# State-space layers on one core: the products h*C of three channel tiles as one GpSimd instruction, and their sum two slots later

## The chip, the cores and the metric

The kernel runs on one core of one Trainium2 chip, everything in float32. The metric is the device time of one launch in microseconds (us). Before the change it is 25216.62 us, the median of three runs (25214.65 to 25219.68).

Names in the profile: PE is TensorE (PEld is its loading of weights, which overlaps with it), DVE is VectorE, ACT is ScalarE, POOL is GpSimd, SP is SyncE, whose queue issues nearly all DMAs.

## What is computed

Two layers of a visual state-space model, one after the other, on x of 8 images of 64x64 pixels with 192 channels. Each layer normalizes, projects to 384 channels, applies a 3x3 depthwise convolution, and then scans the 4096 pixels of an image in K directions (K = 2 in layer 0, K = 4 in layer 1). The core of it, for each direction:

```python
def step(h, inp):
    u_t, dl_t, B_t, C_t = inp
    dA = jnp.exp(dl_t[..., None] * As[None])
    h = dA * h + (dl_t * u_t)[..., None] * B_t[:, :, None, :]
    y = jnp.einsum('bkdn,bkn->bkd', h, C_t)
    return (h, y)
```

h has 384 channels times 16 states. The y of the directions are summed, layer-normalized, multiplied by a gate and projected back to 192 channels.

## The kernel before, in words

Each layer has a front (normalization, projection, convolution, copies to DRAM) and a scan part. The change is in the scan part only, the function `scans`.

**Steps.** A step is 512 pixels of one direction of one image, all 384 channels (three channel tiles of 128 partitions, `dt` = 0, 1, 2) and all 16 states (eight pairs, `m` = 0 to 7). Layer 0 has 8 x 2 x 8 = 128 steps, layer 1 has 8 x 4 x 8 = 256.

**Slots.** A step has 24 slots, one for each pair of a state pair and a channel tile: slot s is m = s // 3, dt = s % 3. Slots are numbered on through the steps; slot 31 of a step is slot 7 of the next one. The loop at the end of `scans` goes through all slots g and issues, in this order and into the in-order queue of each engine:

- `scan(g)`: two recurrences of 128x512 on DVE (L772), one for each state of the pair, reading the decays `da` from SBUF and the inputs `hb` from PSUM and writing the states `h`; behind them, on GpSimd, the product of these two states with C, `hc[:, dt]` from `h[:, dt]` and `cr` (L773);
- the work that two tables, L0_SLOTS and L1_SLOTS, put into this slot (below);
- `inject(g + 2)`: 16 PE instructions (L728) that make the inputs `hb` of the slot two ahead in one of two PSUM buffers, so that they can't start before the scans of slot g are done;
- `decay(g + 4)`: two exponentials on ACT (L745) into one of five buffers `da`, and in all but the first step of a direction a copy (L753) of the entry state, which GpSimd scales in `enter` (L665).

**The sum over states.** `reduce(i, m, n)` adds the products of state n of pair m into the PSUM tile `py` (three channel tiles) with 32x32 matmuls by a mask (L151, a helper). It is put at slot 3m + `slots["reduce"][n]` of its step: 3m + 5 for both n in layer 0, 3m + 5 and 3m + 6 in layer 1. `keep_y` copies `py` to SBUF on ACT (L821) and stores it, at slot 29, that is slot 5 of the next step; there is one `py`, so the next step's first sum waits for that copy. `carry` (L778, ACT, slot 3m + 3) keeps the last state of a chunk for the next one.

**What else has a place in the tables.** All other small PE products of the scan part share a single PSUM bank (tag "m"): each waits until ACT or DVE has read the one before. These are, with their slots in layer 0 / layer 1, counted from the step before the one that they serve: `x_proj` (L568) - / 1, 1, 3; `turn_b` (L594) 3 / 6 with the ACT copy `keep_b` (L605) at 4 / 8; `dt_proj` (L616) for dt = 0, 1, 2 at 7, 0, 4 / 5, 8, 10 with the ACT pass `dt_bias` (L630) at 8, 2, 5 / 6, 10, 11; `turn_delta` (L683) at 12, 15, 14 / 14, 15, 13 with the DVE product `make_dut` (L691) at 13, 17, 15 / 15, 16, 14. `add_y` (L151, not in the bank) adds the earlier directions to `py` at 12 / 13 (in one of the four directions of layer 1 at 24).

A finished image is closed in chunks, the operations `f_...`: once in two steps in layer 0, once in four in layer 1. Their PE parts (L871 gate, L896 and L911 sums, L950 output) lie in layer 0 at slots 9, 10, 18 twice, 22 twice (gate), 20 and 30 (sums), 23 and 32 (totals), 42 three times, 44, 46 twice (output); in layer 1 at 11, 12, 17, 18, 20, 22 (gate), 41 and 67, 45 and 70, 83, 84 twice, 89, 91, 94. Their DVE parts are two passes of 128x1536 (L914, L925; slots 24 and 33 / 48 and 72) and two additions (L959). On GpSimd they have three products of 128x512 (L944, `f_times`), at 38, 39, 36 / 76, 79, 72.

**Buffers.** `h` of one state pair (all three channel tiles, 128x3072) has two buffers, `hc` of the same size three, `cr` three. `load_c` (L714) loads `cr` of pair m at slot 3m - 6 and waits on the SP queue until GpSimd has read the buffer's last user, pair m - 3.

Of the kernel before, what the change touches and what calls it, by code (L numbers as in the profile page):

```python
# [8 lines left out]
F32 = mybir.dt.float32  # L9
# [6 lines left out]
P = 128  # L16
# [8 lines left out]
DT = 3  # L25
NS = 16
T = 512
# [27 lines left out]
    "turn_delta": (12, 15, 14),  # L55
    "make_dut": (13, 17, 15),
    "softplus": 10,
    "reduce": (5, 5),
    "add_y": 12,
    "add_turned": 26,  # L60
    "keep_y": 29,
    "f_norm": 8,
    "f_gate": ((9, 10), (18, 18), (22, 22)),
    "f_keep": (11, 20, 23),
# [37 lines left out]
    "turn_delta": (14, 15, 13),  # L102
    "make_dut": (15, 16, 14),
    "softplus": 11,
    "reduce": (5, 6),
    "add_y": 13,
    "add_turned": 24,
    "keep_y": 29,
    "f_norm": 6,
    "f_gate": ((11, 12), (17, 18), (20, 22)),  # L110
    "f_keep": (13, 19, 24),
# [399 lines left out]
def scans(tc, name, x_src, x_dst, xcd, xcd_col, xtd, xdd, t, dirs, rank, row_b, gate, slots, last, consts, dram):  # L511
# [5 lines left out]
    nc = tc.nc  # L517
# [27 lines left out]
    with tc.tile_pool(name=f"{name}_s1", bufs=1) as s1, tc.tile_pool(  # L545
        name=f"{name}_s2", bufs=2
    ) as s2, tc.tile_pool(name=f"{name}_psy", bufs=1, space=PSUM) as psy, tc.tile_pool(
        name=f"{name}_psh", bufs=2, space=PSUM
# [7 lines left out]
        live = {}  # L556
# [199 lines left out]
        def scan(i, s):  # L756
            m, dt = divmod(s, DT)
            b, k, cols, rev, ci, c = steps[i]
            hb, da = live[i].pop(("hb", s)), live[i].pop(("da", s))
            if dt == 0:  # L760
                live[i]["h", m] = (
                    s2.tile([P, DT, 2, T], F32, name="h"),
                    s2.tile([P, DT, 2, T], F32, name="hc", bufs=3),
                )
            h, hc = live[i]["h", m]
            for n in range(2):
                o, a = h[:, dt, n], da[:, n]
                v = hb.rearrange("p r (j n) -> p n (r j)", n=2)[:, n]
                if rev:
                    o, a, v = o[:, ::-1], a[:, ::-1], v[:, ::-1]  # L770
                init = 0.0 if ci == 0 else 1.0
                nc.vector.tensor_tensor_scan(o, a, v, init, ALU.mult, ALU.add)  # L772
            nc.gpsimd.tensor_mul(hc[:, dt], h[:, dt], live[i]["cr", m])  # L773

        def carry(i, m):
            b, k, cols, rev, ci, c = steps[i]
# [301 lines left out]
        with tc.manual_schedule(engines=ENGINES):  # L1078
            g = min(todo)
            while todo:  # L1080
                i, s = divmod(g, NSL)
                if 0 <= g < N * NSL:
                    scan(i, s)
                for f, a in sorted(todo.pop(g, []), key=lambda fa: rank_of.get(fa[0], 1.5)):
                    f(*a)
                if 0 <= g + 2 < N * NSL:
                    inject(g + 2)
                if 0 <= g + 4 < N * NSL:
                    decay(g + 4)
                g += 1  # L1090
# [113 lines left out]
```

## Time and profile before

| | |
|---|---|
| median of three runs | 25216.62 us |
| the profiled execution: its span | 25231.1 us |
| its scans, layer 0 (128 steps) | from 961.3 us to 8928 us, 62.2 us for a step |
| its scans, layer 1 (256 steps) | from 9864.6 us to 25183 us, 59.8 us for a step |
| busy, PE / DVE / ACT / POOL, 12000 to 24000 us | 11572.89 / 11429.45 / 9435.76 / 11526.37 us of 12000 |
| busy, the same, 3000 to 6000 us | 2855.39 / 2832.74 / 2388.18 / 2833.29 us of 3000 |

The profiled execution is known by its span, 14.5 us (0.06%) above the median of the runs. In a row of instructions, "x9216 | 21566.7, 2368 | 2985.7" means 9216 instructions, busy 21566.7 us together, 2368 ns each, and 2985.7 us of idle time of the engine just before them. In a timeline, a row is a time from the span's start, a length, an engine, and what it did how often; the bracket is the idle time before it and what ended it. A PE operation that shows x16, x24 or x48 is a bundle of instructions of one slot.

### The profile page before, as it was taken

To read this page: it belongs to the slowest core of one execution; us is meant where nothing else is said; L and a number is where in the kernel's file an instruction comes from. 1 tells how busy PE (TensorE), PEld (TensorE's weight loads), DVE (VectorE), ACT (ScalarE), POOL (GpSimd) and SP (SyncE) were. 2 spreads that over 40 slices of the span, in tenths; PEclk is the share of its full clock that TensorE was granted. 3 is DMA by queue.
4 is the path that set the end of the run, shared out by engine and by line. 5 is a ranking of instruction groups with operands and counts; after the bars stand their busy time and mean duration, and the time that the engine had idled before them with its cause. 6 is when DMAs were issued, how large, how long until landed. Compare 5 with 4: busy or idle time off the path is not lost.

```text
span 25231.1 us, 794569 instructions
## 1 busy us (share of the span) xinstructions
PE 24024.7 (95%) x340032; PEld 13528.4 (54%) x340032; DVE 23345.8 (93%) x22142; ACT 19452.6 (77%) x37140; POOL 22144.2 (88%) x10287
## 2 busy tenths in 40 slices
PE   9999999999999999999999999999999999999999
PEld 4555555555555544555555555555555555555554
DVE  7899999999999777999999999999999999999998
ACT  5677788778878767777777777777777777777777
POOL 0499999999999713999999999999999999999998
PEclk9999999999999999999999999999999999999999
DMA  4566666666666555675675575675675575576575
GB/s 161 154 158 158 158 158 159 156 158 159 160 158 159 138 179 195 170 164 168 170 166 168 170 165 169 169 165 169 170 163 170 170 164 169 170 163 171 167 166 143
DMA packets 3836413, 4141.15 MB, mean 164 GB/s; under 512 B 2140460, under 2 KB 2340804, under 8 KB 3829828
## 3 DMA queue, kind: packets, MB, share of 16 engines
q1 hardware_dynamic: 3821296, 4032.72, 61.7%
q8 instruction: 2693, 44.12, 0.8%
q10 hardware_dynamic: 11604, 57.59, 0.6%
q14 instruction: 820, 6.72, 0.1%
HBM read 3443.63 MB, written 645.99 MB: 162 GB/s over the span
## 4 chain that ended last, share of the span: by engine, by line
PE 50%; DVE 25%; ACT 19%; issue 5%; DMA 1%; POOL 0%; SPq 0%; DVEq 0%; ACTq 0%; POOLq 0%
DVE h L772 22%; PE hb L728 20%; PE py L151 14%; ACT da L745 8%; PE pt L616 3%; PE pd L568 2%; PE pc L151 2%; PE po L950 2%; PE pz L871 2%; ACT delta L144 2%; ACT L144 1%; ACT L640 1%; PE pi L322 1%; ACT da L753 1%; ACT delta L630 1%
## 5 line engine op out<-in xcount | busy, mean ns | idle before, releaser
L773 POOL TENSOR_TENSOR hc<-h,cr 128x1024 f32<-128x1024 f32 x9216 | 21566.7, 2368 | 2985.7 <-DMA xt_k<-xtd 1844.7
L772 DVE TENSOR_TENSOR_SCAN h<-da,hb 128x512 f32<-128x512 f32 x18432 | 20860.2, 1199 | 1262.2 <-PE hb L728 1038.8
L745 ACT ACTIVATE da<-delta,a_neg 128x512 f32<-128x512 f32 x18432 | 12249.7, 713 | 1763.7 <-DVE h L772 1736.3
L728 PEld LDWEIGHTS hb<-dg,dut 64*128 64x128 f32 x147456 | 9215.4, 185 | 6720.3 <-issue 5785.3
L728 PE MATMUL hb<-dg,dut 64*128 64x128 f32 x147456 | 10835.6, 286 | 603.9 <-DVE h L772 413.0
L151 PE MATMUL py<-hc,mask 32*32 32x512 f32 x147456 | 6866.8, 601 | 36.0 <-ACT y L821 32.7
L151 PEld LDWEIGHTS py<-hc,mask 32*32 32x32 f32 x147456 | 1582.8, 103 | 2359.7 <-issue 1722.2
L753 ACT COPY da<-a 128x2 f32<-128x2 f32 x8064 | 1562.5, 194 | 293.9 <-ACT da L745 1.8
L778 ACT COPY st<-h 128x6 f32<-128x6 f32 x2688 | 537.4, 200 | 1142.3 <-DVE h L772 1140.0
L616 PE MATMUL pt<-xdbl,w_dt 96*128 96x512 f32 (+1 forms) x2304 | 1302.2, 646 | 38.8 <-DVE yc L914 15.9
L630 ACT ACTIVATE delta<-pt,dtb 128x512 f32<-128x512 f32 x1152 | 787.2, 683 | 449.5 <-PE pt L616 444.4
L355 DVE SCALAR_TENSOR_TENSOR tp<-pad,cw,tp 128x512 f32<-128x512 f32 x1344 | 988.2, 750 | 113.0 <-ACT tp L349 78.9
L683 PE MATMUL pq<-ident,delta 128*128 128x128 f32 x4608 | 758.7, 287 | 324.4 <-DVE dut L691 226.6
L871 PE MATMUL pz<-xn_sq,w_in 96*128 96x512 f32 x1536 | 835.3, 643 | 42.0 <-ACT g L882 27.2
L691 DVE TENSOR_TENSOR dut<-pq,xt_k 128x512 f32<-128x512 f32 x1152 | 767.7, 666 | 83.4 <-PE pq L683 83.4
L568 PE MATMUL pd<-x_k,w_x 128*128 128x512 f32 x1536 | 798.3, 629 | 35.8 <-DVE yc L914 15.1
L950 PE MATMUL po<-yc,w_out 128*96 128x512 f32 x1536 | 783.0, 621 | 16.2 <-POOL yc L944 13.3
L683 PEld LDWEIGHTS pq<-ident,delta 128*128 128x128 f32 x4608 | 484.2, 141 | 522.0 <-DVE dut L691 342.9
L151 PE MATMUL pc<-pad,taps 32*32 32x512 f32 x13824 | 577.9, 592 | 17.1 <-ACT xo L370 13.4
L821 ACT COPY y<-py 128x1536 f32<-128x1536 f32 x384 | 551.7, 1437 | 35.7 <-PE py L151 19.4
L144 ACT ACTIVATE delta<-delta 128x1536 f32<-128x1536 f32 x384 | 570.4, 1485 | 4.3
L944 POOL TENSOR_TENSOR yc<-yc,g 128x512 f32<-128x512 f32 x384 | 490.0, 1279 | 79.1 <-ACT yc L935 72.9
(105 smaller groups left out, 10143.1 us busy)
## 6 DMA issues: line engine op xcount, KB each, us to landing
cr<-cscr SPq DMA_DIRECT2D x2048, 512.0 KB, 4.4
dg<-dgd SPq DMA_DIRECT2D x1536, 512.0 KB, 7.9
cr<-xdd SPq DMA_DIRECT2D x1024, 512.0 KB, 6.4
xt_k<-xtd SPq DMA_DIRECT2D x768, 384.0 KB, 7.1
xcd<-xo SPq DMA_DIRECT2D x128, 768.0 KB, 3.5
xtd<-xv SPq DMA_DIRECT2D x128, 768.0 KB, 4.4
y<-yrow SPq DMA_DIRECT2D x128, 768.0 KB, 5.0
yc<-yrow SPq DMA_DIRECT2D x128, 768.0 KB, 7.2
```

Source lines behind the costliest of these rows:

```text
L144: nc.scalar.activation(out, in_, AF.Softplus)
L151: nc.tensor.matmul(out[j * Q : (j + 1) * Q, dt], w[i * Q : (i + 1) * Q], x[i * Q : (i + 1) * Q], start=first, stop=last, tile_position=(i ...
L568: nc.tensor.matmul(live[i]["pd"][:R], w_x[:, dt, k, :], live[i]["x"][:, dt], start=(dt == 0), stop=(dt == DT - 1),)
L616: nc.tensor.matmul(pt, w_dt[:, k, dt * P : (dt + 1) * P], live[i]["xdbl"][:rank], start=True, stop=True,)
L683: nc.tensor.transpose(pq[:, g], live[i]["delta"][:, dt, g * P : (g + 1) * P], ident)
L728: nc.tensor.matmul(hv[:, r, q], live[i]["dut"][r * G : (r + 1) * G, dt, q], dg[r * G : (r + 1) * G, q, :, 2 * mm : 2 * mm + 2], start=True ...
L745: nc.scalar.activation(da[:, n].rearrange("p (r g j) -> p r g j", r=2, j=G), live[i]["delta"][:, dt].rearrange("p (g r j) -> p r g j", r=2 ...
L753: nc.scalar.copy(da[:, :, f], live[i]["a0"][:, dt, 2 * m : 2 * m + 2])
L772: nc.vector.tensor_tensor_scan(o, a, v, init, ALU.mult, ALU.add)
L773: nc.gpsimd.tensor_mul(hc[:, dt], h[:, dt], live[i]["cr", m])
L871: nc.tensor.matmul(fin["pz"], w_in[:, u, dt * P : (dt + 1) * P], fin["xn"][:, u], start=(u == 0), stop=(u == CT - 1),)
L950: nc.tensor.matmul(fin["po"][:CP], w_out[:, dt, u * CP : (u + 1) * CP], fin["y"][:, dt], start=(dt == 0), stop=(dt == DT - 1),)
```

## The change

The product with C is no longer issued for each slot. It is issued once for a state pair, when the third channel tile has been scanned, as one GpSimd instruction of 128x3072 in which `cr` is repeated for the three channel tiles. `h` gets three buffers in place of two, `hc` two in place of three (each has the same size, so the sum stays). The sums `reduce` move two slots later, and `keep_y` one slot later.

```diff
 L0_SLOTS
-    "reduce": (5, 5),
+    "reduce": (7, 7),
-    "keep_y": 29,
+    "keep_y": 30,
 L1_SLOTS
-    "reduce": (5, 6),
+    "reduce": (7, 8),
-    "keep_y": 29,
+    "keep_y": 30,
...
             if dt == 0:
                 live[i]["h", m] = (
-                    s2.tile([P, DT, 2, T], F32, name="h"),
-                    s2.tile([P, DT, 2, T], F32, name="hc", bufs=3),
+                    s2.tile([P, DT, 2, T], F32, name="h", bufs=3),
+                    s2.tile([P, DT, 2, T], F32, name="hc"),
                 )
...
                 nc.vector.tensor_tensor_scan(o, a, v, init, ALU.mult, ALU.add)
-            nc.gpsimd.tensor_mul(hc[:, dt], h[:, dt], live[i]["cr", m])
+            if dt == DT - 1:
+                cr = live[i]["cr", m].unsqueeze(1).to_broadcast([P, DT, 2, T])
+                nc.gpsimd.tensor_mul(hc, h, cr)
```

## The prediction

> **What bounds the kernel now.** I read the page's table of groups, then who waited for whom, then timelines of single slots. The groups give the durations and show three engines nearly full:
>
> ```profile
> L773 POOL TENSOR_TENSOR hc<-h,cr 128x1024 f32<-128x1024 f32 x9216 | 21566.7, 2368 | 2985.7 <-DMA xt_k<-xtd 1844.7
> L772 DVE TENSOR_TENSOR_SCAN h<-da,hb 128x512 f32<-128x512 f32 x18432 | 20860.2, 1199 | 1262.2 <-PE hb L728 1038.8
> L944 POOL TENSOR_TENSOR yc<-yc,g 128x512 f32<-128x512 f32 x384 | 490.0, 1279 | 79.1 <-ACT yc L935 72.9
> ```
>
> Busy shares don't say who sets the pace; the waits do:
>
> ```profile
> POOL hc L773 <- DVE h L772: 1095.9, 1553, 8.6
> DVE h L772 <- PE hb L728: 1038.8, 1773, 8.7
> PEld py L151 <- POOL hc L773: 233.0, 342, 1.8
> DVE h L772 <- ACT st L778: 84.0, 141, 1.7
> ```
>
> GpSimd waits for the scans, the scans wait for PE's `hb`, and never for GpSimd. (The 1844.7 us in the first row are two long gaps, the fronts.) So the pace is set by DVE, and where DVE idles, by PE. The timeline of layer 0 around slot 20 of a step shows how. First PE, then DVE:
>
> ```profile
> 3996.80 1.06 PE L896 MATMUL ps<-yc,mean_w 128*32 128x512 f32 x6
> 3997.78 2.21 PE L151 MATMUL py<-hc,mask 32*32 32x512 f32 x48
> 3999.93 2.13 PE L728 MATMUL hb<-dg,dut 64*128 64x128 f32 x32
> 4001.99 1.98 PE L871 MATMUL pz<-xn_sq,w_in 96*128 96x512 f32 x4
> ```
>
> ```profile
> 3996.02 4.55 DVE L772 TENSOR_TENSOR_SCAN h<-da,hb 128x512 f32<-128x512 f32 x4 [0.50 <-PE hb L728]
> 4001.24 6.78 DVE L772 TENSOR_TENSOR_SCAN h<-da,hb 128x512 f32<-128x512 f32 x6 [0.67 <-PE hb L728]
> 4007.94 1.73 DVE L914 TENSOR_TENSOR yc<-yc,pm 128x1536 f32<-128x1536 f32 x1
> ```
>
> In one slot PE has the sums (`py` x48, 2.15 us to the next start) and another product (`ps`, 0.98); the inject behind them is late, and the scans of slot 22 start 0.67 us late. Every slot so crowded costs DVE time. The change moves the sums to other slots, so I count them.
>
> **PE's account.** DVE needs 2.22 us for a slot (x6 in 6.78, x4 in 4.55: 2.23 for two scans). PE needs 1.12 for the inject, which leaves 1.10 for other work W. An inject can't start before the scans two slots back end, so it can be early by little: 2.22 less the 0.09 by which scans overlap, 1.19 for the inject and some 0.25 for the two hand-overs, about 0.70. So: slack = min(0.70, slack + 1.10 - W); below zero, DVE waits that long and the slack is zero. DVE's own extra pieces (`dut` 0.59, `yc` 1.65, `xr` 0.59) are added to the slack where they lie. W in us: two sums 2.14, one 1.05; `dt_proj`, `x_proj`, gate, total 1.06 (two of a kind 1.9); chunk sum 0.99; output 1.03, 1.89, 2.75 for one to three; `turn_delta` 0.59; `turn_b` 0.35. Alone, a slot up to W = 1.8 is free.
>
> Two waits at the shared bank belong in it. In layer 0 `dt_proj` in slot 0 waits for `yc` (L914), so that slot ends 0.25 short. In both layers `turn_delta` in a slot in which DVE also makes the `dut` before it starts late: 0.81 + 0.59 - W remains at most if another `dut` follows, else 0.81 - W.
>
> *Layer 0, two steps.* Before, sums in slots 2, 5, 8, ... The waits are 0.25, 0.34, 0.34, 0.30, 0.34, 0.81 (slot 18, output), 0.97 (slot 20), 0.54 in one step, and three times 0.34, 0.96 (slot 11), 0.56 (18, gate), 1.33 (20), 0.11, 0.45 in the other: 8.3 us. After, sums in slots 1, 4, 7, ..., beside `dt_proj` at 4 and 7, gate at 10 and 22, output at 46. In one step 0.25, 1.04 (slot 1, right behind the late slot 0), 1.40 (4), 1.40 (7), 0.29, 0.23, 1.00, 1.64 (22), in the other 0.34, 1.40 (4), 1.40 (7), 1.40 (10), 0.29, 0.23, 0.75, 2.25 (22): 15.3 us. That is +7.0 for two steps; without a chunk (4.1 to 9.4) +5.3.
>
> *Layer 1, four steps.* Before, sums in slots 2, 5, ... and 3, 6, ...: beside `x_proj` 3.3, `dt_proj` and `turn_b` 3.7, `turn_delta` 1.9, the chunk 5.6; 14.5 us. After, sums in slots 1, 4, ... and 2, 5, ... One meets `x_proj` in slot 1 (W = 2.97: 2.3 in all), and in slot 13 one meets `turn_delta` and `add_y` (2.69: 2.6). A new wait comes too: the last sum now lies in slot 5, so the copy `keep_y` (1.44 on ACT) at slot 6 waits for it; behind it on ACT stand a `carry` (0.2), the decays and `dt_bias` (0.68), and `turn_b` on PE in slot 6 needs the bank that `dt_bias` empties. 1.44 + 0.2 + 0.68 less the inject's 1.12, with hand-overs, is 1.3 us of PE. Slots 5 to 10 then cost 9.8 in place of 3.7. With 1.0 for slot 14 and 4.6 for the chunk: 20.3 us, +5.8 for four steps; without a chunk (9.9 to 17.6) +1.9 for one.
>
> *Sum.* Layer 0: 55 pairs x 7.0 + 10 steps x 2.65 = 412. Layer 1: 56 fours x 5.8 + 25 steps x 1.9 = 372. Together 785. **Check on before:** in 1700 to 8400 us the waits of L772 are 337 us in some 110 steps, 3.1 a step, where the account has 4.2; in 10800 to 24500, 649 in 229 steps, 2.8 where it has 3.6. It is a quarter too high, and 785 becomes 590 at the low end. I take the middle, 690.
>
> **The other parts.**
> - *GpSimd.* Removed: 9216 x 2368 ns. Added: 3072 of 128x3072. Rows for 512 and 1024 elements differ by 1089 ns for 512, so 3072 take 1279 + 5 x 1089 = 6.72 us as a line, at most 3 x 2.37 = 7.1. That saves 0.4 us for a state pair, 1.2 ms of GpSimd's time, at an engine that nobody waits for but `py`: I count nothing of it on the path. Cover: a product now begins when the third scan ends and takes 2.7 slots; PE comes to the sum some 4.5 slots after that end, so nearly 2 are left.
> - *Rule of the Trainium skill against this.* GpSimd is busy 11526 of 12000 us (12000 to 24000), DVE 11429. Perfetto Trace Analysis, "Identifying the Most-Contended Engine", takes the engine with the highest occupancy as the one to optimize, and does not trust matmul occupancy on PE. By it GpSimd would be that engine, and the 1.2 ms would come off the time (about 24000 us); by the waits they come off nothing.
> - *Three `h`.* Of the 84 us of DVE waits for `carry`, 0 to 84 go; I take 30, since most stand where PE is late as well. *Two `hc`.* The next but one product waits for the sum of its buffer, which in layer 1 ends about when that product may start; a loss up to 0.5 us is within GpSimd's 0.9 spare for a state pair: 0.
> - *PE's 233 us for `hc`*, 0.7 each, about the slack: 0 to 233 gained; I take 0.
> - *The `f_times`* (1.28 us) and `enter` (0.25) now queue behind 6.7 us. In the last seven steps of layer 0 two of them stand behind the product of slot 20, and the output products in slot 22 wait some 2 slots: 7 x 2 x 2 = 28, of which I take 20, PE being late there anyway.
> - *SP's queue.* `load_c` holds it until GpSimd frees `cr`, now 4.4 us later. All loads behind are later by up to that: `xdbl` (landing 7.2 us, needed about 2.5 us after) has the least left. 0, or see below.
>
> 690 + 20 - 30 = +680 on the profiled execution (span 25231.1); the median is 14.5 less, which changes a difference by nothing: 25217 + 680 = **25900 us**.
>
> **Rivals.**
> 1. *Faster*: the backlog of GpSimd is what delays PE and thus the scans, and DVE's slack swallows the crowding. Then the 233 and the 84 us go, and little comes: 25217 - 317 = 24900. For it: 96% busy. Against: DVE's waits name PE, and 0.50 and 0.67 us stand exactly behind crowded slots. It decides once crowding costs under 317 us, under half of the account's low end. Chance 0.11.
> 2. *The same*: old crowding (slots 18, 20, 23) goes as new comes, within 50 us. For it: PE's total work is unchanged. Against: `dt_proj` at 4 and 7 and `turn_b` are in every step. Chance 0.05.
> 3. *Slower still*: a load comes late. `xdbl` missing its use by 2.4 us in all 128 steps of layer 0 adds 307: 26200. Chance 0.10.
>
> That the one instruction is no cheaper than three (7.1) changes nothing while it stays under the 7.5 us of three slots; beyond that GpSimd would be the bound (in 0.10 too).
>
> **Range.** Crowding forecast 0.74. Low: 590 less 84 and most of the 233: some +290, 25500; high: 785 + 28 + 307 = +1120, 26330. With a little of rival 1: 25450 to 26330. Faster by over 0.2% (50 us, about what can be told from no change) 0.11, within 0.05, slower 0.84.
>
> **What would show it.** `DVE h <- PE hb` grows from 1039 to about 1700 us, most in the scans of slots 6, 9 and 0 in layer 0 and of 3, 8, 10 in layer 1; `turn_b` (L594) waits for `delta` (L630) in layer 1; the product has 3072 instructions of some 6.7 us and GpSimd idles more; `DVE h <- ACT st` is gone. If DVE's waits for PE do not grow, the account is wrong; if new waits name a DMA, rival 3 holds.

## The result and the profile after

The changed kernel takes 26882.17 us (median of four runs, 26871.54 to 26903.01) against 25218.15 us of the kernel before beside it: 1.0659 times, 95% interval 1.0644 to 1.0674. That is 1664 us slower. The forecast was 25900 us, slower by 680, in a range that ended at 26330. The sign was right, the size was not.

The groups of the page, and who waited for whom, in the profile of the changed kernel (span 26869.6 us):

```profile
L775 POOL TENSOR_TENSOR hc<-h,cr 128x3072 f32<-128x3072 f32 x3072 | 20655.1, 6730 | 5516.5 <-PE py L151 2855.3
L772 DVE TENSOR_TENSOR_SCAN h<-da,hb 128x512 f32<-128x512 f32 x18432 | 20907.3, 1200 | 2815.7 <-PE hb L728 2481.7
```

```profile
POOL hc L775 <- PE py L151: 2855.3, 1617, 10.7
DVE h L772 <- PE hb L728: 2481.7, 2312, 7.6
PEld pb L594 <- ACT delta L630: 356.6, 256, 2.4
PE pb L594 <- ACT delta L630: 303.0, 256, 1.2
PE py L151 <- DMA y<-ycol: 95.0, 46, 4.5
DVE h L772 <- ACT st L780: 12.0, 40, 0.6
```

GpSimd does its products in 20655 us, 912 less than before (6.73 us for each, where 6.72 were forecast), and now waits for PE. DVE's waits for `hb` have grown by 1443 us, from 1039. Two waits are as good as new: `turn_b` (L594) for `dt_bias` (L630), 256 times, once in each step of layer 1, and PE's `add_y` for the loads `y<-ycol`. The scans' wait for `carry` has all but gone, from 84 us to 12.

Where the time came from is seen best by kinds of steps. The table gives the mean time from the first scan of a step to that of the next, from the trace's scan instructions. "Turned" are the 64 steps of layer 1 that read their earlier sum across the other direction; "last" are the steps that close the chunks of the last image.

| us for a step | before | after | steps | together |
|---|---|---|---|---|
| layer 0, without a chunk | 58.5 | 63.5 | 8 | 40 |
| layer 0, with chunks | 61.4 | 68.2 | 112 | 762 |
| layer 0, last | 81.3 | 87.3 | 6 | 36 |
| layer 1, ordinary | 59.2 | 61.5 | 184 | 420 |
| layer 1, turned | 60.4 | 65.2 | 64 | 312 |
| layer 1, last | 70.7 | 76.6 | 7 | 41 |

The last column is from unrounded means; its sum is 1611 of the 1638.5 us by which the two spans differ. Layer 0 has lost twice what the account of slots gave it, and the turned steps stand out in layer 1.

A third thing shows in a timeline of PE over the turn of two steps in layer 0 of the changed kernel, and in the granted clock (the number after the busy times of PE, PEld, DVE, ACT and POOL) of stretches of it:

```profile
5137.20 1.19 PE L728 MATMUL hb<-dg,dut 64*128 64x128 f32 x16
5140.39 1.21 PE L616 MATMUL pt<-xdbl,w_dt 12*128 12x512 f32 x2 [2.00 <-DVE yc L916]
5141.53 2.08 PE L728 MATMUL hb<-dg,dut 64*128 64x128 f32 x16
5143.54 2.77 PE L151 MATMUL py<-hc,mask 32*32 32x512 f32 x48
5146.24 2.12 PE L728 MATMUL hb<-dg,dut 64*128 64x128 f32 x32
5148.29 0.42 PE L594 MATMUL pb<-ident,xdbl 16*128 16x16 f32 x4
5150.06 1.19 PE L728 MATMUL hb<-dg,dut 64*128 64x128 f32 x16 [1.35 <-DVE h L772]
5151.18 1.76 PE L616 MATMUL pt<-xdbl,w_dt 12*128 12x512 f32 x2
5152.87 3.95 PE L151 MATMUL py<-hc,mask 32*32 32x512 f32 x48
5156.75 2.84 PE L728 MATMUL hb<-dg,dut 64*128 64x128 f32 x32
```

```profile
5136.00:5138.00 2.00, 2.00 (x19) 1.11 (x19) 1.64 (x2) 0.00 (x0) 2.00 (x1) 1.00 0.90 111
5141.00:5145.00 4.00, 4.00 (x47) 2.25 (x50) 2.85 (x4) 3.94 (x8) 1.11 (x2) 0.57 1.02 213
5152.00:5158.00 6.00, 6.00 (x62) 2.17 (x62) 2.36 (x3) 3.24 (x5) 2.18 (x2) 0.50 0.40 97
```

PE stands for 2.00 us, until `yc` is read out of the shared bank, and just after that gets 0.57 of its clock. The same two sums (`py` x48) that took 2.21 us at full clock take 2.77 and, after a second idle time of 1.35 us, 3.95. Over the middle of layer 0 the granted clock is 0.99 before (first row) and 0.95 after (second):

```profile
2600.00:8500.00 5900.00, 5613.35 (x79698) 3320.18 (x79698) 5560.61 (x5066) 4704.16 (x9006) 5567.30 (x2605) 0.99 0.65 158
```

```profile
2600.00:8500.00 5900.00, 5288.52 (x72145) 3068.07 (x72144) 5042.97 (x4587) 4285.78 (x8161) 4842.07 (x978) 0.95 0.59 143
```

So there were three suspects beside each other: the crowded slots of the forecast, the clock, and late loads; and the long product itself as a rival to all three. In the expectations, the figures "by the account" (4.1 us a step in layer 0, 2.0 in layer 1) are the forecast's account with all waits at the shared bank carried through, worked out after the result.

### The profile page after: what moved, and what is told of

It is laid out like the page before. It is cut to its first block, busy times and chain, and to the rows that moved or that the text cites. A ratio compares the mean times of both kernels' runs of the same rounds, so it can differ in the third digit from the quotient of the medians.

```text
span 26869.6 us, 788459 instructions
## 1 busy us (share of the span) xinstructions
PE 24535.6 (91%) x340032; PEld 13687.6 (51%) x340032; DVE 23395.9 (87%) x22142; ACT 19482.2 (73%) x37140; POOL 21257.4 (79%) x4143
## 4 chain that ended last, share of the span: by engine, by line
PE 31%; DVE 14%; ACT 10%; issue 3%; SPq 2%; DMA 2%; POOL 2%; DVEq 0%; ACTq 0%; POOLq 0%
PE hb L728 12%; DVE h L772 12%; PE py L151 9%; ACT da L745 4%; PE pd L568 3%; PE pt L616 3%; POOL hc L775 1%; ACT y L823 1%; SPq L807 1%; ACT delta L630 1%; PE pc L151 1%; PE pz L873 1%; DMA y<-ycol 1%; DVE dut L691 1%; ACT delta L144 1%
## 5 line engine op out<-in xcount | busy, mean ns | idle before, releaser
L775 POOL TENSOR_TENSOR hc<-h,cr 128x3072 f32<-128x3072 f32 x3072 | 20655.1, 6730 | 5516.5 <-PE py L151 2855.3
L772 DVE TENSOR_TENSOR_SCAN h<-da,hb 128x512 f32<-128x512 f32 x18432 | 20907.3, 1200 | 2815.7 <-PE hb L728 2481.7
L151 PE MATMUL py<-hc,mask 32*32 32x512 f32 x147456 | 7058.5, 619 | 2.9 <-POOL hc L775 2.9
L630 ACT ACTIVATE delta<-pt,dtb 128x512 f32<-128x512 f32 x1152 | 790.3, 686 | 422.8 <-PE pt L616 422.8
L151 PE MATMUL py<-y,mask 32*32 32x512 f32 x6144 | 505.2, 729 | 106.2 <-DMA y<-ycol 95.0
```

The lines of the kernel that those rows point to most:

```text
L151: nc.tensor.matmul(out[j * Q : (j + 1) * Q, dt], w[i * Q : (i + 1) * Q], x[i * Q : (i + 1) * Q], start=first, stop=last, tile_position=(i ...
L630: nc.scalar.activation(live[i]["delta"][:, dt].rearrange("p (g r j) -> p r g j", r=2, j=G), live[i]["pt"].rearrange("p (r g j) -> p r g j" ...
L775: nc.gpsimd.tensor_mul(hc, h, cr)
```

## The experiments

Each time stands beside the kernel before on the same chip; its ratio has the interval behind it.

**1. The slots without the product.** On the kernel before:

```diff
-    "reduce": (5, 5),
+    "reduce": (7, 7),
...
-    "reduce": (5, 6),
+    "reduce": (7, 8),
...
-    "keep_y": 29,
+    "keep_y": 30,
```

> The kernel before with the sums and the copy keep_y in the slots of the change, and nothing else: three products of 128x1024, two h, three hc. Crowding theory (the slots cost, not the one instruction): layer 0 goes from 61.4 to about 66 to 68 us a step, ordinary steps of layer 1 from 59.2 to about 61.2, so at least 25218 + 125 x 4.1 + 250 x 2.0 = 26230 us; with the low TensorE clock that the changed kernel shows in layer 0 about 26600. Rival (the long product and the two hc cost: its start waits for the third scan and for the sum): with short products the time stays within 0.5% of 25218. Late-load theory: the steps that load the turned directions stay near 60.4 + 2 = 62.5 us, below the 65.2 of the changed kernel, as cr is freed early here.

Measured 26526.91 us, 1.0523 [1.0505, 1.0540]. Layer 0 with chunks takes 68.0 us, ordinary steps of layer 1 61.3, turned ones 61.8. So 1314 us of loss come from moving the sums and `keep_y`, with not one product changed. The turned steps stay quick, as the late-load theory wanted. The rival falls as an explanation of the whole. The other 350 us or so came with the long product; experiments 6 and 10 find 252 and 46 of them. And not all of the 1314 us is crowding on PE: with two `h`, up to 191 us are scans that wait for GpSimd to be done with the buffer. In the changed kernel, with three, the same wait is 2.6 us.

```profile
DVE h L772 <- POOL hc L773: 191.0, 111, 2.9
```

**2. The product without the slots.** On the changed kernel, the lines of experiment 1 reversed (sums in 5, 5 and 5, 6; `keep_y` at 29).

> The changed kernel with the sums and keep_y back in the old slots: one product of 128x3072, three h, two hc. Crowding theory: no new crowded slot; the sums wait a little for the product, which ends 2.7 slots after its third scan while PE comes there 2.4 to 3 slots after it. By the account layer 0 +1.5, layer 1 +0.9 us a step: about 25640 us, and the turned steps may still be late. Rival (the long product costs): above 26500 us.

Measured 25973.79 us, 1.0303 [1.0287, 1.0318]: 330 above the expectation, 530 below the rival's line. Layer 0 takes 63.2, ordinary steps of layer 1 60.9. The waits say why:

```profile
PEld py L151 <- POOL hc L775: 1459.5, 1716, 5.4
PE py L151 <- POOL hc L775: 683.7, 1151, 4.5
```

In the old slots PE comes to the sums before the long product is done (233 us before the change, for all of the first kind). So the sums did have to move; the question is where to.

**3. Layer 0's sums apart.** On the changed kernel:

```diff
-    "reduce": (7, 7),
+    "reduce": (7, 8),
```

> The changed kernel with layer 0's two sums of a state pair in slots 7 and 8 in place of both in 7. Crowding theory: no slot of layer 0 has two sums beside another product; by the account 3.7 us less for a step of layer 0, 470 us, and the low clock there mostly goes as PE's idle time before slot 1 is followed by less work: 26000 to 26450 us, layer 1 unchanged. Rival (product and buffers cost): within 100 us of 26880.

Measured 26070.28 us, 1.0341 [1.0326, 1.0357]: 812 us less than the changed kernel for one sum moved by one slot in layer 0. Layer 0 with chunks takes 61.5 us, as before the change (61.4); layer 1 stays (61.5). More than the account's 470 us went, and the clock came back with it, to 0.99. How much of the gain is slots and how much is clock, this run alone can't say.

```profile
2600.00:8000.00 5400.00, 5151.78 (x73240) 2835.44 (x73238) 5101.40 (x4656) 4304.21 (x8266) 4914.79 (x989) 0.99 0.65 158
```

**4. The idle time in slot 0 taken away.** On the changed kernel:

```diff
-    "dt_proj": (7, 0, 4),
+    "dt_proj": (7, 1, 4),
```

> The changed kernel with dt_proj of tile 1 in slot 1 in place of slot 0 in layer 0, so that PE does not sit idle for 2.0 us until the shared bank is read by L916. The account of slots: the late slot 0 (0.25) goes and slot 1 becomes as crowded as slot 4 (1.40 in place of 1.04): no change, within 50 us of 26880. Clock theory (the idle time of PE halves its clock for 3.4 to 10 us just after, in 52 + 47 places of layer 0): these halvings go, and with them 2.5 to 5 us in each of 56 pairs of steps: 26600 to 26740 us, mean clock above 0.985.

Measured 26862.98 us, 1.0654 [1.0638, 1.0670]: no change that the intervals tell apart, and the clock theory missed. But its premise failed too: the mean clock is 0.979 against 0.977. The spells of half clock, which lay nearly all in one step of each pair, now begin in both. The two steps of a pair changed from 72.7 and 63.8 us to 68.1 and 67.6. The run doesn't tell the theories apart.

**5. The idle time filled.** On the changed kernel, sums by a zero mask, which add zeros, where PE idles in layer 0 (slots 24 to 35 of step e of each chunk are slots 0 to 11 of the step after it):

```diff
+    "fill": (24, 24, 27, 33, 35),
...
+        zero = s1.tile([P, Q], F32, name="zero_w")
+        nc.vector.memset(zero, 0.0)
...
+        def fill(i):
+            for dt in range(DT):
+                w = w_out.rearrange("p t c -> p (t c)")[:, :T]
+                block_diag(nc, live[i]["py"], zero, w, dt, False, False)
...
+                for q in slots.get("fill", ()):
+                    at(e, q, fill, e + (q > 30))
...
+                    (fill,),
```

> The changed kernel with five blocks of sums by a zero mask into py for every closed chunk of layer 0, where PE sits idle: two in slot 0 of the even step ahead of the dt_proj that waits 2.0 us for the shared bank, one each in its slots 3, 9 and 11. They add 5 x 1.05 us of PE's work for a pair of steps and nothing to the result. Account of slots: no gain, a loss of 0.3 us or more for a pair, 26880 to 26950 us. Clock theory (idle PE is given half its clock right after): the half-clock time of layer 0 falls from 1000 us by about half, and the time by 140 to 220 us: 26660 to 26740 us.

Measured 26697.86 us, 1.0589 [1.0574, 1.0605]: 184 us less, with more work. Layer 0 with chunks goes from 68.2 to 66.6 us. The stretch that had 0.95 has

```profile
2600.00:8500.00 5900.00, 5483.69 (x79235) 3124.64 (x79218) 5160.47 (x4697) 4390.64 (x8348) 4958.66 (x997) 0.98 0.60 146
```

PE got more work, and nothing else was changed; what changed in PE's favour is the clock, by 0.03 of 5900 us (177 us) in this stretch. So the clock is shown to be a cause. About half of its loss went here: 184 us of the some 350 that are estimated for 126 steps of layer 0 below (2.8 us a step).

**6. Four cr.** On the changed kernel:

```diff
-            cr = s2.tile([P, 2, T], F32, name="cr", bufs=3)
+            cr = s2.tile([P, 2, T], F32, name="cr", bufs=4)
```

> The changed kernel with four buffers of cr in place of three, so that the SP queue no longer stands until the product of three pairs back ends. Late-load theory (the 64 steps of layer 1 that load the turned directions take 65.2 us, ordinary ones 61.5, because the twelve loads of y stand behind load_c on SP): these steps fall to about 62 us, 64 x 3.3 = 210 us less: 26660 us; layer 0 and the ordinary steps as they are. Rival (these steps are slow for the slots alone): within 50 us of 26880.

Measured 26630.14 us, 1.0561 [1.0545, 1.0577]: 252 us less. The turned steps fall from 65.2 to 61.7 us, 64 x 3.5 = 227 us; ordinary ones stay (61.4). The SP queue's longest waits, before the change, in the changed kernel and with four `cr`:

```profile
SPq L714 <- POOL hc L773: 11834.1, 2281, 13.1
```

```profile
SPq L714 <- POOL hc L775: 13158.3, 2106, 17.0
```

```profile
SPq L714 <- POOL hc L775: 7231.3, 1458, 15.3
```

The twelve loads of a turned `y` are put into slots 8 to 19, between the `load_c` that hold the queue until a product is done. The queue stood nearly as long in total before the change, with shorter single waits (13.1 us at most, against 17.0), and a turned step took 60.4 us; so the total is no sign of late loads, the steps are. The waits of `add_y` for `y<-ycol` are no longer among the longest. Late loads are shown.

**7. Two h, three hc.** On the changed kernel:

```diff
-                    s2.tile([P, DT, 2, T], F32, name="h", bufs=3),
-                    s2.tile([P, DT, 2, T], F32, name="hc"),
+                    s2.tile([P, DT, 2, T], F32, name="h"),
+                    s2.tile([P, DT, 2, T], F32, name="hc", bufs=3),
```

> The changed kernel with two h and three hc, as before the change. GpSimd's product waits 2855 us for the sums of the buffer that it reuses; theory: that wait costs nothing as the product is not late, so within 0.3% of 26880. Rival (the two hc delay products, sums and with them cr): at least 200 us less, in the turned steps above all.

Measured 26826.18 us, 1.0639 [1.0624, 1.0655]: 56 us less, within what was expected; the intervals of the two ratios overlap. GpSimd's 2855 us of waiting for `py` are the largest of its waits and cost next to nothing. Ordinary steps of layer 1 are a little longer (61.6 us), the turned ones shorter (64.1).

**8. dt_bias ahead of keep_y.** On the changed kernel, in layer 1:

```diff
-    "dt_proj": (5, 8, 10),
-    "dt_bias": (6, 10, 11),
+    "dt_proj": (4, 8, 10),
+    "dt_bias": (5, 10, 11),
```

> The changed kernel with dt_proj of tile 0 and its dt_bias one slot earlier in layer 1 (4 and 5), so that dt_bias stands ahead of keep_y on ACT. New-wait step of the prediction (turn_b waits 1.3 us for dt_bias behind keep_y, 256 times): the 660 us of PE's waits for delta before turn_b go, and by the account 0.8 us of a step of layer 1: 200 us less, 26680 us. If that wait was hidden: within 50 us of 26880.

Measured 26677.29 us, 1.0580 [1.0563, 1.0598]: 205 us less. Ordinary steps of layer 1 go from 61.5 to 60.7. In the changed kernel PE and PEld wait side by side for `dt_bias`, here in a step of layer 1:

```profile
14013.33 0.41 PE L594 MATMUL pb<-ident,xdbl 16*128 16x16 f32 x4 [1.20 <-ACT delta L630]
14013.33 0.32 PEld L594 LDWEIGHTS pb<-ident,xdbl 16*128 16x128 f32 x4 [1.40 <-ACT delta L630]
```

That wait, which stood at 356.6 us for PEld and 303.0 for PE, is now

```profile
PEld pb L594 <- ACT delta L630: 4.8, 2, 2.4
PE pb L594 <- ACT delta L630: 1.6, 2, 0.8
```

**9. Three mendings together.** The edits of 3, 6 and 8 on the changed kernel.

> The changed kernel with three mendings together: layer 0's sums in slots 7 and 8, four cr, and dt_proj and dt_bias of tile 0 a slot earlier in layer 1. If they are three separate losses, their gains add: 26882 - 812 - 252 - 205 = 25610 us, some 400 us above the kernel before, most of it in ordinary steps of layer 1 (60.6 against 59.2). If they hide one another, above 25750 us. If the one product brought a gain once the slots suit it, below 25400 us.

Measured 25646.08 us, 1.0169 [1.0152, 1.0186]. 812 + 252 + 205 = 1269 were to go and 1236 went: three separate losses.

**10. The last products of layer 0 earlier.** On 9, in L0_LAST:

```diff
-    "f_affine": (19, 20, 20),
-    "f_times": (19, 20, 20),
+    "f_affine": (19, 19, 19),
+    "f_times": (19, 19, 19),
```

> The same with the last two affine passes and GpSimd products of the closing chunks of layer 0's last image in slot 19 in place of 20, so that they stand ahead of the long product of slot 20. These six steps take 87 us against 81 before the change; if the wait of the output products behind the long product is the cause, they fall to about 81 us: 40 us less than the run beside it. Otherwise no change.

Measured 25600.5 us, 1.0153 [1.0138, 1.0168]: 46 us less, and the last steps of layer 0 go from 87.6 to 80.5 us. The wait behind the long product was their loss; it is the steps that show it, for the intervals of the two ratios overlap.

**11. Three products in the mended slots.** On the kernel before, the slots of 9 and four `cr`.

> The kernel before (three products of 128x1024, two h, three hc) in the slots and with the four cr of the first run of this call. Theory: the one product is worth nothing either way once its sums lie two slots later, but for 45 us in the last steps of layer 0: within 60 us of the first run less 45. Rival (the long product costs, or saves, GpSimd's time on the path): more than 150 us away from it.

("The first run" is experiment 9; "less 45" brings it to experiment 10.)

Measured 25762.46 us, 1.0213 [1.0198, 1.0228]: 116 us above 9, where 45 below it were expected. My theory that the one product is worth nothing missed. Layer 1 is the same (60.5); layer 0 with chunks takes 63.1 us against 61.7. Against experiment 10, where the wait behind the long product is gone as well, the one product with its buffers saves some 160 us once the slots suit it. The granted clock differs too, here (first row) and in experiment 10 (second):

```profile
2600.00:8500.00 5900.00, 5567.08 (x77834) 3060.66 (x77822) 5427.10 (x4947) 4583.05 (x8788) 5442.80 (x2544) 0.98 0.63 154
```

```profile
2600.00:8500.00 5900.00, 5604.57 (x79318) 3079.56 (x79308) 5529.67 (x5042) 4667.70 (x8953) 5323.64 (x1072) 0.99 0.66 157
```

What the product, the buffers and the clock each have in the 160 us was not taken apart.

**12. Sums three slots later.** On the changed kernel, with four `cr` and the edit of 10:

```diff
-    "reduce": (7, 7),
+    "reduce": (8, 8),
...
-    "reduce": (7, 8),
+    "reduce": (8, 9),
...
-    "keep_y": 30,
+    "keep_y": 31,
+    "load_y": 8,
...
-                at(i, 6, load_y, i)
+                at(i, slots.get("load_y", 6), load_y, i)
```

(`keep_y` and `load_y` change in layer 1 alone; `load_y` stays behind `keep_y`, which uses its buffer.)

> The changed kernel with the sums three slots later than before the change in place of two (8, 8 in layer 0; 8, 9 in layer 1, keep_y of layer 1 at 31 and its load_y at 8), four cr, and the products of layer 0's last chunks a slot earlier. A state pair has three slots, so every sum again lies beside the same other products of PE as before the change. Crowding theory: layer 0 back to 61.4 us a step, layer 1 to 59.9 to 60.7, few halvings of the clock: 25250 to 25450 us, below the 25600 of the version with mended slots. If being late itself costs (products and sums far behind the scans, two hc): above 25600 us.

Measured 25537.63 us, 1.0126 [1.0109, 1.0143]: the best of the versions with the long product, though 90 us over what was expected and still above the kernel before. Layer 0 with chunks is at 61.5 us, its value before the change. Ordinary steps of layer 1 are at 60.0, turned ones at 61.4. Being late costs layer 0 nothing; what cost was that both sums landed beside other work. (In experiment 3 one of the two is late by no multiple of three, and layer 0 takes 61.5 us as well.) What keeps layer 1 0.8 us above its old 59.2 was not taken apart.

## Why the prediction was right and wrong

- *What bounds the kernel*: right. DVE fed by PE sets the pace, not GpSimd. GpSimd's busy share fell from 88% to 79% while the time rose by 6.6%. By the rule of the Trainium skill that the prediction weighed and set aside (Perfetto Trace Analysis, "Identifying the Most-Contended Engine": the engine with the highest occupancy first), the time would have fallen; it rose, and rival 1 falls with it.
- *Crowded slots*: the right mechanism, shown by experiments 1, 3 and 12, but mis-sized: the sum has 690 us for it, and moving the sums and `keep_y` alone cost 1314 (experiment 1). The step that failed is the one behind "It is a quarter too high, and 785 becomes 590 at the low end. I take the middle, 690". The account was made smaller, where it had to be made larger. In layer 0 it gave 3.5 us a step (7.0 for two); measured are 6.8. The waits of L772 that were set against it, 3.1 us a step in layer 0, leave part of the lost time out. A step with chunks took 61.4 us before, and DVE's own work in it, by the account's prices, is 57.3 (24 x 2.22, 3 x 0.59 and half of 2 x 1.65 + 2 x 0.59); the difference, 4.1, is what the account had (4.2). And a check on a kernel with few crowded slots could not see what crowding does to the clock.
- *What layer 0 lacked*: the clock, which no term of the sum had. By the rows above, 1 - 0.95 of 5900 us are 295 us of PE's clock in 87 steps, 3.4 us a step; before it was 59 us in 95 steps, 0.6. The difference, 2.8, and the account's 3.5 make 6.3 of the 6.8; this is an estimate, from rounded rows and as if all of the lost clock were on the path. Experiment 5 shows 1.6 of it by filling idle time alone. The account counts PE's durations as constant; the same two sums took 2.21 us before and 2.77 and 3.95 in the timeline after.
- *Layer 1*: the account gave 1.45 us a step (5.8 for four), ordinary steps lost 2.3, with short products as with long ones (experiment 1). The new wait of `turn_b` was foreseen at its place and time (1.3 us; 356.6 us of PEld and 303.0 of PE in 256 steps are 1.4 and 1.2, side by side); undoing it brings 0.8 a step. The rest was mis-sized, and I can't say by which slot.
- *SP's queue*: "0, or see below" failed. Loads do come late, but not `xdbl` in layer 0: the turned `y` of layer 1, which I did not name, for 227 us (experiment 6). Rival 3 had the right mechanism, 307 us, at the wrong place, as an alternative with a chance of 0.10, where it was a term that came on top. The forecast had nothing for it.
- *`f_times` behind the long product*: 20 us were taken of 28; 46 are measured (experiment 10).
- *GpSimd counted at nothing*: nearly right. In the changed kernel nothing of its 912 us is seen; in slots that suit it, the product, its buffers and the clock together bring some 160 us (experiment 11).
- *Three `h`, two `hc`*: right for the waits, not for the time. 72 of the 84 us of waits for `carry` went, but the sum's gain of 30 us is not seen: with the old buffers the changed kernel is 56 us faster, if anything (experiment 7; the intervals overlap), its ordinary steps of layer 1 0.1 us longer and its turned ones 1.1 shorter.
- *Range*: its upper end summed the account, `f_times` and one late load (785 + 28 + 307) and still ended 550 us short. Most of that is layer 0, whose steps lost 838 us (762 + 40 + 36) where 412 + 28 were counted: the clock had no term.

## What to carry to other kernels

In a schedule written by slots, a batched instruction moves its consumers, and what counted here, in layer 0 at least, is which other work they land beside, not how late they are: shift them by a whole period, or count the new neighbours slot by slot. Follow all that a longer instruction holds: the buffers that it frees later, the queue that waits for them, and the small pieces behind it on its own engine. When PE is nearly the bound, treat its idle time of a microsecond or two as a cost of its own, and add a term of the same sign to the forecast instead of holding it as an alternative.

## What the runs showed of the hardware

In this kernel TensorE's granted clock falls to half after short idle times. In layer 0 of the changed kernel 228 such spells begin, 3.4 to 10 us long and together 911 us; before it was 25 and 137 us. They begin whole multiples of 3.413 us apart. The longest idle time of PE around the start of a spell is 1.35 us in the median and 2.0 us in 19 of 20 at most.

The Trainium skill, TensorE: Matmul & The Clock Gate, Part 1: The HAM clock gate (the "warmup" mystery), names an activity window of about 3.4 us and lets an idle window of that length bring the half clock. The lengths of the spells agree with such a window (3.413 us and its multiples). The idle times that came before them are shorter than such a window, so here one that was only partly idle was enough. In the 3.413 us before a spell PE was busy, by its rows in the trace, for 53% in the median and for 80% at most (86% before the change). Cut layer 0 of the changed kernel into stretches of 3.413 us in step with the spells: after a stretch in which PE was busy for more than 80%, no spell began; after one with less, some did and some did not.
